# A hybrid block on one core: a re-planned instruction order, a fifth convolution on TensorE, and a routing in two branches

## The chip, the cores and the metric

The kernel runs on one core of a Trainium2 chip. The metric is the device time of one execution in microseconds. A core has five engines with their own in-order instruction streams: TensorE (PE) multiplies matrices, VectorE (DVE) and ScalarE (ACT) work element by element, GpSimd (POOL) does the same and helps out, and SyncE (SP) issues nearly all DMA transfers. Engines wait for one another through semaphores, so an instruction whose input is late holds everything behind it on its own engine.

## The reference

The input x is 8 sequences of 512 tokens with 128 features. Four residual layers follow one another, each on a layer-normalised input:

- attention A: a gated delta rule over 16 heads of size 8. Queries, keys and values are projections of the input, each followed by a causal convolution of four taps in time and a SiLU. A state of 8 x 8 per head is carried from token to token: `v_new = (v - k S) * beta; S = S + outer(k, v_new); o = q S`.
- a mixture of experts (MoE): logits over 8 experts, the two largest chosen, their softmax weights normalised; each expert is relu(x W1) W2 with W1 128 x 256 and W2 256 x 128. The reference computes all 8 experts for all tokens and weighs them.
- attention B: linear attention with elu + 1 as its feature map, causal, with a state of 8 x 9 per head from chunk to chunk.
- the same MoE again, with the same weights.

## The kernel before, in words

**Units.** The 512 tokens are cut into 8 units (`c`, 0 to 7) of 64 time steps (`CH`) of all 8 sequences: 512 tokens each, four tiles of 128. For each unit, in this order: `prepare` (layer norm, projections with convolution, normalised keys), `recurring` (the delta rule), `ending` (its output, written by the VectorE instruction `on` and passed over DRAM by two DMAs, `sco` and `oT`), then `f` (the first MoE), `b` (attention B) and `g` (the second MoE). The last unit is split into two halves from `f` on.

**The delta rule.** `recurring` walks through 16 steps of four tokens per unit. Each step is a chain of four VectorE instructions: `pj` (product), `factors` (sum), `terms` (product), `st` (sum), and the next step needs the `st` of this one. `substituted` prepares the four tokens of a step so that they can be taken together (its tiles are `W`, `spare` and `near`). GpSimd multiplies the outputs (`po`); they are summed by TensorE in the first three units, by VectorE in the others.

**Entering the MoE.** When `on` has come back through DRAM, TensorE multiplies it by the output weights (`s_po_a`, in `add_projected`) and VectorE adds it to x. That is the first TensorE instruction of `f`.

**The MoE.** For each expert, TensorE computes `s_ph` (two matmuls of 512 columns), ScalarE the relu (`hT`), TensorE `y_py` (two matmuls). The scaled input of an expert (`wt_xsT`) is made by GpSimd from weights that a DMA spreads over all partitions (`scw`). Expert weights lie in eight buffers `resident_0` to `resident_7`.

**The convolution.** With `TAPS_ON_PE = 4`, units 0 to 3 are convolved on TensorE: `weights_of_taps` multiplies the projection by each tap, and `convolved` issues four matmuls (`s_pp_a<-xnT_a,resident`) per projection. Units 4 to 7 are convolved by one matmul, two ScalarE instructions and three VectorE `scalar_tensor_tensor` per projection (`s_pp_a<-cv_a`). The tap weights `wc` lie in `resident_5` to `resident_7`, so that `loading_later_weights` must wait for the last tap matmul of unit 3 before it loads experts 5 to 7.

**Routing.** In `moe`, `first_of_largest` finds the largest logit and a one-hot mark of it, twice; then `relative` makes the two weights from the difference of the two largest logits (subtract, scale, tanh on ScalarE, two more on VectorE).

**Attention B.** In `attend`, GpSimd makes outer products of keys and values in the buffer `kv` (two instructions `kv_b`), TensorE sums them causally (`s_pc_b`), and VectorE multiplies by the queries (`qs_b`, `nd_b`).

**The order.** Nothing is scheduled on the chip, and the instruction order is not written out by hand either. The class `Weaver` runs the whole kernel as generators that name the engine of their next step, and takes at each point the generator that can start first, with ties and small differences decided by `chains` (length of work behind a step) and by offsets in `FAVOURED` and `OFFSETS`. Start times come from the prices in `duration()`, plus extra time booked by `weaver.took(...)`. `PLANS = 4` plans are made without instructions, and the last one fixes the order. The prices thus decide which instruction stands where on its engine; on the chip each engine then follows that order.

**Fill.** Where the planner sees TensorE idle for 0.6 us or more, `keep_busy` (line 1950) issues matmuls of ones by ones that compute nothing, for 0.7 of the gap, so many at a price of 0.22 us each. The profile shows them as `busy`.

Of the kernel before, what the change touches and what calls it, by code (L numbers as in the profile page):

```python
# [19 lines left out]
P = 128  # L20
# [17 lines left out]
TURNED = 1  # L38
# [3 lines left out]
TAPS_ON_PE = 4  # L42
# [4 lines left out]
ADDED_ON_DVE = (4,5,6,7)  # L47
NEAR_NORMS = (5,6,7)
# [5 lines left out]
TURNED_IN = (0,7)  # L54
# [13 lines left out]
PASSES = ()  # L68

FAVOURED = {  # L70
    ("b", 0.0): 1475, ("b", 1.0): -605, ("b", 2.0): 408, ("b", 3.0): -1141, ("b", 4.0): 1159, ("b", 5.0):
    -397, ("b", 6.0): -3095, ("b", 7.0): -2237, ("b", 7.5): -2071, ("beside",): 1509, ("ending",): 696,
    ("f", 0): 1839, ("f", 1): 922, ("f", 2): 673, ("f", 3): -941, ("f", 4): 1648, ("f", 5): 1050, ("f", 6):
    -1587, ("f", 7): 767, ("f", 7.5): -2892, ("g", 0.0): 1576, ("g", 1.0): 901, ("g", 2.0): 357, ("g", 3.0):
    7212, ("g", 4.0): -253, ("g", 5.0): -2424, ("g", 6.0): -246, ("g", 7.0): 1986, ("g", 7.5): -2626,
    ("outputs",): 7, ("prepare", 0): -904, ("prepare", 1): -3306, ("prepare", 2): 224, ("prepare", 3):
    -1571, ("prepare", 4): -839, ("prepare", 5): -16, ("prepare", 6): 680, ("prepare", 7): -2427, ("recur",
    0): 3219, ("recur", 1): -6342, ("recur", 2): -2844, ("recur", 3): 482, ("recur", 4): -2744, ("recur",
    5): -1405, ("recur", 6): 1064, ("recur", 7): -724, ("values",): 149, None: -1498,
# [4 lines left out]
    -5735, -5206, -179, -62, -5753, 0, -6219, -6323, 29, -6838, 1464, 2372, 2338, -2, 1277, -3446, -3136,  # L84
    2417, -3137, -2112, -3119, -3650, -311, 76, 1, 3, -3, 77, -342, -7970, 977, -20, -4091, 3665, -19, 806,
    -4343, -4621, -4648, -4379, 711, 806, -5289, 1734, 1900, 1275, 623, -5269, -420, -380, -832, -1479, 50,
    -758, -790, 125, -3620, 585, -553, 237, 2322, 2064, -5521, 501, -5381, -5928, -3498, -40, 2563, 4086,
    10628, -5495, 782, 11097, 2142, 524, -2998, -175, 1440, -9862, 334, 747, 94, -5047, -6796, 307, 308,
    -1787, -402, -3506, -63, -187, 265, -2927, -6059, -6411, -6618, 0, -4528, -6371, -6553, -6091, -5056,
    263, -538, -1107, -6503, -6983, -6, -6510, -36, -961, -967, 294, 389, -6742, -8230, -142, -7747, -8737,  # L90
    -7250, -7254, -7665, -422, 1935, 282, -996, -6683, -9031, 177, 1221, 466, 360, -7342, 552, -8817, -42,
    -7371, 101, 1699, 247, 245, 186, -7410, 57, 713, -5151, 127, -91, -80, -5933, 56, -6006, -6402, 412,
    -6116, -445, 35, 2434, -4925, -4928, -4874, -938, 1079, 406, -7960, 775, 519, -186, -183, -6551, -7752,
    -7695, -8113, 429, 2079, 1870, 73, 72, 717, 130, -428, -37, 347, 2267, 385, -69, 3340, -640, -367, 165,
    -831, -1483, 0, 486, -5539, -200, -199, -399, -34, 2547, -7582, -106, -2671, 11037, 1388, 1383, 1120,
    -962, 17, -1270, -6162, -175, -5673, 211, 50, -7246, -2444, -7484, -2599, -386, 24, -1456, -1295, -1542,
    449, 95, 3319, -2490, -5181, -17, 250, 1245, 968, 926, -3459, -1, -51, -7241, -6288, -40, -5786, 456, 0,
    2, -7292, 471, -361, -79, -6239, 1121, 209, 228, 171, -490, -335, -1339, -4313, -4533, -173, -162,
    -1885, -4676, -5235, -6460, -342, -6601, -6575, 266, 235, 4646, 4647, 78, -899, -7489, 388, -348, 4,
    2051, 1488, -3366, -170, -1594, -5834, -4738, -590, -6081, 2703, 771, 806, 2101, -1052, -4471, -334,  # L100
    10046, 384, -6869, -6546, 10224, -8058, 323, -1252, 463, 8950, 0, -8361, 1480, -113, -361, -8416, -9767,
    -47, -200, -9523, 27, -8517, -60, 66, -8349, -229, -9575, -9613, 177, 0, -516, 2087, 1808, 1102, -3472,
    -3462, -3444, -261, -48, -604, -199, 8924, -1499, -2626, 0, -5333, -68, 0, -3882, -1964, 1388, 1387,
    -3692, -5022, -5065, -555, 136, 6558, 1420, 1897, 1801, 9994, 299, 277, 324, -41, 8082, 391, 7156, 7157,
    -5841, -322, -1273, -5351, 627, 9366, -2233, -2747, 1391, 674, -7825, -11438, -30, 775, 2023, 1821,
    -1660, -376, -7698, 679, -3112, 1424, -5849, 0, -55, 151, -899, 680, -7529, -8147, 148, 896, 1077, 914,
    339, 108, 425, -1456, -5019, -1472, -477, 2580, -4207, -3854, -4163, -8696, -1145, -4645, -48, -435,
    -49, -441, -2007, 528, -6603, 2721, 2590, 71, 790, 1764, 678, -1104, -11, -8403, -631, -307, -17, 8979,
    -26, 111, 125, -3643, 387, 709, -7661, -6188, -1529, 52, -267, -2256, -1638, -163, -7464, -7718, -7716,
    -1060, 1984, -7251, 341, -416, 74, 246, 826, 0, -1331, 114, -9262, 817, -794, -1132, -4670, 22, 677,  # L110
    -1102, -247, -991, 5324, 1460, 7056, -68, 22, -4777, -5911, -267, -245, 0, -5384, 611, 1441, -3227,
    -3228, 7000, -4910, -4927, 8594, 7076, 656, 8970, 534, 0, -414, -452, 8696, 199, -1793, 526, 7399,
    -2385, -2142, -2082, 703, 601, -344, 673, 889, 675, -225, 700, 0, 1159, -2605, -52, 1613, 16, -121, 10,
    3158, 128, 131, -45, -73, 1613, -6492, -6728, -6847, 1627, -162, 2762, 283, 57, -585, 605, 1, -6681,
    -6644, -7468, 1614, -1785, -6492, 3296, -2793, 740, 1374, 1438, -5170, -5140, 909, 2571, -5016, 298,
    -5165, -4644, -50, -42, -4475, 2, 294, -85, -2740, -6839, 226, 1693, -57, 3901, -15, 128, 27, -353,
    1777, -988, 548, -1117, 51, -5550, -5713, 147, 12, -34, -4251, 1589, 1915, 47, -3918, 1053, 111, -9287,
    183, -73, -1509, -1272, -1576, 1611, -436, 1, 5846, -1241, -112, 1631, -1205, 1597, 150, -2745, -3535,
    2377, 2411, 1644, 1676, -1215, 1575, -4452, 8420, 702, -792, 816, 406, 430, 763, 8525, 846, -158, 8634,
    8574, 7499, -111, 1400, 1450, 1002, 8654, -2038, 769, 762, 607, 2855, 6551, -97, -90, -87, 5399, 647,  # L120
    -2965, 11537, -1025, 26, 1690, -128, 1901, -2876, -579, -1637, -1629, 2367, 1239, 1591, 19, 1583, 1724,
    11913, 9792, -979, -5647, 234, 2469, -6345, 305, -458, 202, 495, 2179, 331, -2292, 9691, 1045, 6, 9790,
    35, -5846, 323, 577, 1291, 9691, -58, -97, 118, -5, -4, 615, -5886, 76, -98, -106, -3895, 613, 2012,
    -4473, 833, 614, 2011, -59, -171, -3273, -3336, -3353, -3, -4885, 1032, 10012, 4, 9990, -8535, 13, -26,
    -426, 9852, -8409, 100, -8705, 1140, -1782, -3, -354, -197, -1938, -335, 9717, -197, 9802, 2602, -4020,
    6594, -4069, 2798, 3058, 2, -79, -78, 391, 1966, 1709, 200, 8716, 1885, 10615, 11418, 3662, 9797, 2272,
    1035, 2099, 0, 1824, 10195, 9823, 10532, 9755, 10009, 1333, 1142, -251, 8119, 297, 296, 41, 749, 4723,
    747, 1875, 2107, 724, -124, 453, 7278, 3607, 3799, 273, 3441, 3113, -3692, -398, -3768, -334, -3765,
    -3766, -582, -412, 9876, -382, 1211, 10712, -1001, 93, -1201, 9799, -302, 9584, 9796, 780, 9701, -580,
    1068, 9799, -828, -878, 2215, 2732, -4744, 3104, 2677, 2684, 2623, 238, -387, -153, 2284, -614, 2072,  # L130
    231, 2027, -4996, -71, 30, 457, -4797, 384, -249, 4030, 2190, -5523, 4173, 1217, 3083, 1929, -714, 605,
    676, -732, -321, -57, 3956, 733, 11526, -7059, -800, 1502, 239, -723, -808, -318, -541, 8037, -8544, 15,
    -4952, -5089, -5252, -4993, 2029, -304, -831, -5698, -69, -6182, -350, -409, 2461, 257, -282, -7155,
    -5747, 0, -11360, 2325, 2107, 2122, 386, -5700, -3106, -1352, 0, 0, -1541, 372, -1538, -3081, -1573,
    -1435, -66, 3013, -2727, -4066, -895, -131, -4357, 2917, -4077, -498, 0, -3157, -80, -404, -3201, -3374,
    0, 1576, 1292, 11286, -3695, -3696, 11437, 2265, 10445, 11425, 0, 3814, -3061, -6147, -44, -59, 400,
# [331 lines left out]
def duration(key, op, args, kw):  # L468
# [12 lines left out]
    if key == "ACT":  # L481
        table = TABLE_OF.get(args[2]) if op == "activation" else None
        scale = args[2] if op == "mul" else kw.get("scale", 1.0)
        more = (0.19 if "bias" in kw else 0.0) + (0.0 if isinstance(scale, float) else 0.08)
        return key, 0.2 + more + n * 0.76e-3, 0.1, table
# [1523 lines left out]
```

## Time and profile before

| | |
|---|---|
| median of 3 runs | 791.46 us (791.4 to 791.99) |
| profiled execution, its own time | 792.24 us |
| its span, first to last instruction | 790.5 us |
| mean granted TensorE clock | 0.989 |
| PE / DVE / ACT / POOL busy | 761.7 / 565.3 / 504.4 / 446.1 us |
| PE fill (`busy`), 195 matmuls | 54.4 us |
| DMA | 59.67 MB, 75 GB/s in the mean |

The page gives busy time by engine, the span in 40 slices, a chain of the work that ended last, and groups of like instructions. A row of a group reads: line, engine, operation, output and inputs by tile name, shapes, count, then busy time and the mean duration of one in ns, then the idle time just before them and what ended it. Almost all instructions carry line 454, a helper that records every operation; so groups are told apart by tile names. A tile that begins with `s_` or `y_` lies in a matmul bank. Windows give busy time within stretches that the reader chooses; waits list who waited for whom. An fp32 matmul shows as two records.

### The profile page before, as it was taken

How to read it: one execution, taken by the hardware profiler on the slowest of the kernel's cores; microseconds unless marked ns; L12 is line 12 of the kernel's file. 1: busy time of each engine (PE TensorE's matmuls, PEld its weight loads, DVE VectorE, ACT ScalarE, POOL GpSimd, SP SyncE). 2: the span in 40 equal slices, each digit the busy share in tenths (PEclk: the TensorE clock that was granted, in tenths of full speed). 3: DMA queues.
4: the chain of work that ended last, by engine and by line, in shares of the span. 5: the costliest groups of instructions: out<-in, count | busy, mean ns of one | idle time of the engine just before them, and what ended most of it. 6: DMA issues, size and time to landing. Idle time of an engine off the chain costs nothing.

```text
span 790.5 us, 11578 instructions
## 1 busy us (share of the span) xinstructions
PE 761.7 (96%) x3383; PEld 385.6 (49%) x3383; DVE 565.3 (72%) x1429; ACT 504.4 (64%) x1388; POOL 446.1 (56%) x609
## 2 busy tenths in 40 slices
PE   8889899997999999999999999999999999999997
PEld 4345455553435434544444435454444457644475
DVE  1689898978997799899999799798557155342310
ACT  5765767687876865678676875773664445643352
POOL 1245447659586495775586664877735606735331
PEclk9999899998999999999999999999999999999999
DMA  2451426105233311214133142232112111311121
GB/s 46 118 130 38 129 57 182 51 22 147 70 91 86 98 56 55 80 55 126 54 110 100 31 105 74 82 105 68 41 41 81 60 28 48 108 69 41 40 60 34
DMA packets 82392, 59.67 MB, mean 75 GB/s; under 512 B 48152, under 2 KB 64152, under 8 KB 82328
## 3 DMA queue, kind: packets, MB, share of 16 engines
q1 hardware_dynamic: 81608, 58.64, 26.5%
q8 instruction: 27, 0.44, 0.2%
q10 hardware_dynamic: 720, 0.28, 0.2%
q14 instruction: 37, 0.30, 0.1%
HBM read 46.52 MB, written 12.39 MB: 75 GB/s over the span
## 4 chain that ended last, share of the span: by engine, by line
PE 76%; DVE 13%; ACT 6%; issue 3%; DMA 1%; POOL 1%; DVEq 0%; SPq 0%; ACTq 0%; POOLq 0%
PE s_ph_f L454 14%; PE y_py_f L454 14%; PE s_ph_g L454 12%; PE y_py_g L454 12%; PE s_pc_b L454 4%; PE s_pp_a L454 4%; PE s_pp_b L454 2%; DVE st L454 2%; PE s_pu_b L454 2%; PE busy L1950 2%; PE s_pS_b L454 1%; DVE pj L454 1%; ACT squares L454 1%; DVE terms L454 1%; DVE W L454 1%
## 5 line engine op out<-in xcount | busy, mean ns | idle before, releaser
L454 ACT ACTIVATE hT_g<-s_ph_g 128x512 f32<-128x512 f32 (+1 forms) x144 | 79.0, 551 | 95.4 <-PE s_ph_g L454 94.5
L454 PE MATMUL y_py_f<-hT_f,resident 128*128 128x512 f32 (+1 forms) x288 | 134.3, 555 | 0.3 <-ACT hT_f L454 0.2
L454 PE MATMUL y_py_g<-hT_g,resident 128*128 128x512 f32 (+1 forms) x288 | 133.3, 553 | 0.3
L454 PE MATMUL s_ph_f<-wt_xsT_f,resident 128*128 128x512 f32 (+1 forms) x288 | 132.6, 555 | 0.8 <-ACT wt_xsT_f L454 0.2
L454 PE MATMUL s_ph_g<-wt_xsT_g,resident 128*128 128x512 f32 (+1 forms) x288 | 131.0, 553 | 0.3 <-POOL wt_xsT_g L454 0.2
L454 ACT ACTIVATE hT_f<-s_ph_f 128x512 f32<-128x512 f32 (+1 forms) x144 | 78.7, 549 | 50.1 <-PE s_ph_f L454 48.7
L454 POOL TENSOR_TENSOR wt_xsT_g<-wt_xsT_g,xn_xnT_g 128x512 f32<-128x512 f32 (+1 forms) x69 | 79.1, 1167 | 37.0 <-DMA wt_xsT_g<-scw_g 26.5
L454 POOL TENSOR_TENSOR po<-st,kq 128x256 f32<-128x256 f32 x128 | 93.9, 763 | 3.3 <-DVE st L454 2.7
L454 POOL TENSOR_TENSOR kv_b<-ph_b,v 128x1152 f32<-128x1152 f32 x32 | 69.2, 2177 | 40.3 <-ACT v L454 27.1
L454 POOL TENSOR_TENSOR wt_xsT_f<-wt_xsT_f,xn_xnT_f 128x512 f32<-128x512 f32 (+1 forms) x69 | 79.6, 1172 | 16.4 <-DMA wt_xsT_f<-scw_f 11.5
L454 DVE TENSOR_TENSOR qs_b<-s_pc_b,ph_b 128x360 f32<-128x360 f32 (+1 forms) x96 | 50.4, 551 | 46.4 <-PE s_pc_b L454 45.8
L454 PEld LDWEIGHTS y_py_f<-hT_f,resident 128*128 128x128 f32 x288 | 50.6, 190 | 47.5 <-issue 40.1
L454 PEld LDWEIGHTS s_ph_f<-wt_xsT_f,resident 128*128 128x128 f32 x288 | 50.5, 191 | 46.7 <-issue 31.1
L454 PEld LDWEIGHTS y_py_g<-hT_g,resident 128*128 128x128 f32 x288 | 50.9, 190 | 44.1 <-issue 35.6
L454 PEld LDWEIGHTS s_ph_g<-wt_xsT_g,resident 128*128 128x128 f32 x288 | 50.9, 190 | 43.7 <-issue 32.0
L454 DVE TENSOR_REDUCE st<-terms 128x64 f32<-128x320 f32 x128 | 61.5, 480 | 12.2 <-ACT terms L454 5.8
L1950 PE MATMUL busy<-ones 128*128 128x512 bf16 x195 | 54.4, 420 | 8.8 <-ACT o L454 2.6
L454 DVE TENSOR_REDUCE factors<-pj 128x32 f32<-128x288 f32 x128 | 58.5, 457 | 6.2 <-ACT factors L454 2.5
L454 DVE TENSOR_TENSOR terms<-factors,kt 128x256 f32<-128x256 f32 x128 | 53.7, 419 | 4.0 <-ACT vn L454 1.0
L454 DVE TENSOR_TENSOR pj<-st,factors 128x256 f32<-128x256 f32 x128 | 53.4, 417 | 4.2 <-ACT factors L454 1.5
L454 ACT COPY terms<-st 128x64 f32<-128x64 f32 x128 | 39.6, 309 | 26.2 <-DVE st L454 24.8
L454 POOL TENSOR_TENSOR pq<-y_a,y_a 128x128 f32<-128x128 f32 x32 | 20.9, 679 | 46.8 <-ACT squares L454 23.7
(270 smaller groups left out, 1342.7 us busy)
## 6 DMA issues: line engine op xcount, KB each, us to landing
wt_xsT_f<-scw_f SPq DMA_DIRECT2D x55, 256.0 KB
wt_xsT_g<-scw_g SPq DMA_DIRECT2D x55, 256.0 KB
scr<-y_a SPq DMA_DIRECT2D x24, 256.0 KB
qk<-scr SPq DMA_DIRECT2D x16, 256.0 KB
x_a<-in_x_dram SPq DMA_DIRECT2D x16, 128.0 KB
vv<-scr SPq DMA_DIRECT2D x8, 256.0 KB
sco<-on SPq DMA_DIRECT2D x8, 256.0 KB
oT<-sco SPq DMA_DIRECT2D x8, 256.0 KB
```

The source lines that it names most:

```text
L454: r = call(*args, **kw)
L1950: nc.tensor.matmul(pt, ones, ones.unsqueeze(1).to_broadcast([P, 4, P]), start=True, stop=True)
```

## The change

Five things are changed:

1. `TAPS_ON_PE` is 5: unit 4 is convolved on TensorE as well.
2. The tap weights lie in `kv`, the buffer of attention B's outer products, in place of the weights of experts 5 to 7. The loading of these experts no longer waits; instead the first `attend` waits for the last tap matmul of unit 4.
3. In the routing, `relative` is started as soon as the second largest logit is known, beside the rest of `first_of_largest`.
4. Prices of the planner are corrected: GpSimd's power function 0.4 + 0.16 per element with nothing booked on top (it was 1.05 and 0.8 more), other GpSimd operations, ScalarE's bias and scale, output products in the first units (0.08 in place of 0.3), two VectorE operations that are slower than their formula, and a burst of weight loads.
5. The order is planned anew: two kinds of passes (`PASSES`) follow the four plans, in which steps are placed backwards from the end, and `FAVOURED` and `OFFSETS` are replaced.

`STATES_ON_PE`, `KEYS_ON_POOL` and the code under them are switched off (empty tuples). `TURNED` names the same parts as before.

```diff
-TURNED = 1
+TURNED = {"f0": 1, "g0": 1, "f7": 1, "g7": 1}
-TAPS_ON_PE = 4
+TAPS_ON_PE = 5
+STATES_ON_PE = ()
+KEYS_ON_POOL = ()
+BURST = NE - 3
-TURNED_IN = (0,7)
-PASSES = ()
+PASSES = ((1, 0.0, {}), (2, 0.1, {}))
 FAVOURED = {
...
 OFFSETS = (
...
-        more = (0.19 if "bias" in kw else 0.0) + (0.0 if isinstance(scale, float) else 0.08)
+        more = (0.1 if "bias" in kw else 0.0) + (0.0 if isinstance(scale, float) else 0.06)
         return key, 0.2 + more + n * 0.76e-3, 0.1, table
     if key == "POOL" and ALU.pow in args:
-        return key, 1.05, 0.1
+        return key, 0.4 + n * 0.16, 0.1
     if key == "POOL":
-        return key, 0.2 + n * (1.72e-3 if n > 512 else 2.0e-3), 0.1
+        if op == "tensor_copy":
+            return key, 0.16 + n * 1.3e-3, 0.1
+        return key, 0.18 + n * (1.73e-3 if n > 512 else 2.15e-3), 0.1
...
-    wc = [resident[NE - 3 + s].rearrange("p (k d) -> p k d", k=4) for s in range(3)]
+    kv_ = const.tile([P, 2, NH, V1, HD], F32, name="kv")
+    taps = kv_.rearrange("p w h e d -> p (w h e d)")[:, 0 : 12 * D].rearrange("p (s k d) -> p s k d", s=3, k=4)
+    wc = [taps[:, s] for s in range(3)]
...
-    kvs = held_in(1, [P, 2, NH, V1, HD], "kv")
+    kvs = Slots(weaver, None, None, "kv", 1, [kv_])
...
         for e in range(NE):
-            if TAPS_ON_PE and e >= NE - 3:
-                yield fired("projected", TAPS_ON_PE - 1, e - (NE - 3))
...
                 sp.dma_start(resident[e][:, to], by)
+                if e >= BURST and to.stop < 2 * NF:
+                    weaver.moves(-LANDS)
...
         pool.tensor_tensor(rs[:, 0], rs[:, 0], mhalf, ALU.pow)
-        weaver.took("POOL", 0.8)
...
             dve.tensor_scalar(nrm[:, s], nrm[:, s], ATT_A_EPS * ATT_A_EPS, None, ALU.max)
+            weaver.took("DVE", 0.3)
...
+                weaver.took("DVE", 0.4 * ns / NS)
...
-                                weaver.took("POOL", 0.3)
+                                weaver.took("POOL", 0.08)
...
         def first_of_largest(p, k):
             m = near(nb) if k else row(f"m{k}")
             yield "DVE"
             dve.tensor_reduce(m, p, AX.X, ALU.max)
+            if k:
+                scales["weights"] = spawn(relative(m1, m))
             yield "DVE"
             dve.tensor_tensor(marked, p, over_experts(m), ALU.is_ge)
...
-        m2 = yield from first_of_largest(lg2, 1)
-        yield from relative()
+        yield from first_of_largest(lg2, 1)
+        yield scales["weights"]
...
         projecting = spawn(project())
         adding = spawn(elus())
+        if c == 0:
+            yield from all_of([fired("projected", TAPS_ON_PE - 1, s) for s in range(3)])
         kv = yield from kvs.take(n)
```

## The prediction

> **What bounds the kernel now.** I read the page first: busy shares by engine, then the span in 40 slices.
>
> ```profile
> span 790.5 us, 11578 instructions
> ...
> PE 761.7 (96%) x3383; PEld 385.6 (49%) x3383; DVE 565.3 (72%) x1429; ACT 504.4 (64%) x1388; POOL 446.1 (56%) x609
> ...
> PE   8889899997999999999999999999999999999997
> ...
> DVE  1689898978997799899999799798557155342310
> ```
>
> TensorE (PE) is busy all the time, but 195 of its matmuls are fill that computes nothing ("busy", line 1950). So I cut the span where PE starts the first product of a new unit (`s_po_a`, at 103.08, 153.87, 204.64 and 263.93 us for units 0 to 3) and asked for PE's busy time in each stretch:
>
> ```profile
> 0.00:103.08 103.08, 90.62 (x424) 0.95 0.36 91
> 103.08:153.87 50.79, 49.95 (x218) 1.00 0.39 107
> 153.87:204.64 50.77, 43.66 (x230) 0.93 0.31 81
> 204.64:263.93 59.29, 57.31 (x252) 1.00 0.32 88
> ...
> 740.00:790.50 50.50, 45.76 (x192) 0.99 0.19 48
> ```
>
> (length, PE busy with its count, granted clock, DMA share, GB/s), and for the fill alone (length, PE busy, weight-load busy, then the same):
>
> ```profile
> 0.00:103.08 103.08, 36.95 (x138) 14.39 (x138) 0.95 0.36 91
> 103.08:153.87 50.79, 3.83 (x14) 1.36 (x14) 1.00 0.39 107
> 153.87:204.64 50.77, 9.21 (x28) 3.22 (x28) 0.93 0.31 81
> ...
> sum 790.50, PE 54.36 PEld 20.45; mean PE 5.44 PEld 2.04
> ```
>
> Idle plus fill I call waste. It is 12.5 + 36.9 = 49.4 us in the first stretch, 4.7 in the second, 7.1 + 9.2 = 16.3 in the third, 2.4 in the fourth, 2.8 from 263.93 to 740 us and 4.7 + 2.8 = 7.5 at the end: 83.1 us. The other 707.4 us are real PE work. After 204.64 us PE hardly stops; a microsecond can be won only in real work, or in the 72.8 us wasted ahead of unit 3.
>
> What PE waits for there is VectorE (DVE). A unit enters PE's work when its recurrence has ended with the instruction `on`, which starts at 95.2, 145.05, 193.31 and 251.20 us for units 0 to 3; `s_po_a` follows 7.9, 8.8, 11.3 and 12.7 us later, over two DMAs. DVE is busy for 64.7, 45.8, 41.5 and 48.5 us of the four stretches that end with `on`. The largest DVE wait of the third:
>
> ```profile
> DVE s_pp_a L454 <- ACT s_pp_a L454: 4.3, 1, 4.3
> ```
>
> **The change part by part.** Durations are of the profiled execution, whose own time is 792.24 us (span 790.5 and 1.7 around it), 0.78 above the median 791.46. I add the change of the span to the median.
>
> *Convolution of unit 4 on TensorE.* The built programs have 12 more four-tap matmuls `s_pp_a` and 3 fewer single ones. The row:
>
> ```profile
> L454 PE MATMUL s_pp_a<-xnT_a,resident 128*128 128x512 f32 x96 | 42.9, 595 | 0.0
> L454 DVE SCALAR_TENSOR_TENSOR s_pp_a<-cv_a,cw,s_pp_a 128x512 f32<-128x512 f32 x36 | 26.8, 749 | 4.9 <-ACT s_pp_a L454 4.5
> ```
>
> Two records make one fp32 matmul, so one is 42.9 / 48 = 0.89 us; the chain of waits has 11 in a row in 9.54, 0.87 each. Nine more at 0.87 are +7.8 us of real work on the bounding engine (7.7 with the 0.86 of `s_ph` in a run, 8.1 with 12 x 0.89 less 3 x 0.86). DVE loses 9 x 0.749 = 6.7 us and a wait of up to 4.3; ScalarE loses three copies of about 0.58 and three scalings of 0.65, 3.7 us, none on PE's path; GpSimd six copies of 0.21. The part pays only through an earlier `on`, below.
>
> *Weights in the buffer `kv`.* Experts 5 to 7 no longer wait for the taps; the first outer product of unit 0's attention waits for the last tap matmul of unit 4. In the built order that matmul stands at 85 us of PE work and the first `s_pp_b` of the attention at 122, so 37 us of PE work cover the wait: nothing. Without that cover, GpSimd would hold its `po` products (0.79 us each) behind the waiting `kv`, and `st` buffers behind those. SP issues the same 379 instructions. The nine loads of these weights move ahead: in the order, three stand between `sco` and `oT` of unit 0, each 0.45 us of SP. `oT` waits there for `sco` to land anyway; if it did not, 1.4 us, once.
>
> *Routing.* Both orders have the same DVE instructions; subtract, scaling and tanh now overlap four operations of 0.19. At most 0.8 us for one of 18 routings, and only where PE waits for it (unit 0's, the last half's). Taken as nothing; bounds 0 and -1.6.
>
> *One more table load* on ScalarE (34 to 35 in the order): 1.28 us on an engine with 36% idle; nothing, +1.3 at most. The Trainium skill (ScalarE: Activation LUTs, What ACT_TABLE_LOAD costs) adds about 1.38 us of drain to each, 2.66 in all. Here the load at 14.40 us follows an activation that ends at 14.39, and the next starts at 15.74, so the drain does not show, and the row's value stands; by the page the bound would be +2.7.
>
> *The order.* Fill falls from 195 to 158: 127 ahead of unit 0's `s_po_a` (138 before), 22 in the second stretch (14), none in the third (28), 2 in the fourth (1), 7 later (14). What the waste becomes I take from DVE, with the durations of its rows summed over the built order up to each `on`. Before, these sums are 70.9, 120.9, 167.1 and 220.3; the busy time to the same points is 0.91 of that, since neighbours overlap. After: 64.7, 122.5, 158.9 and 248.1.
>
> Start: unit 0's keys are convolved in turn with its values; two matmuls stand ahead of the last one that the keys need, 1.7 us later for all that follows (bounds 0, if the table load at 14.40 covers it, and 1.7). `on` of unit 0: 95.2 - 0.91 x 6.2 + 1.7 = 91.3 us. Unit 1: 57.8 x 0.91 + 4.1 idle as before = 56.7 on, 148.0. Unit 2: 36.4 x 0.91 + 6.8 = 39.9 on, 187.9 (183.5 without the 4.3 wait). Unit 3: 89.2 x 0.91 + 9.4 = 90.6 on, 278.5; the order now has the preparation of two further units ahead of it (30 more instructions, 17.7 us) and 14 more of attention (8.7).
>
> PE work ahead of each `s_po_a`, by row sums of the order scaled to the trace (1.06): 53.7, 105.4, 143.3 and 224.2 us. Waste up to unit 0: 91.3 + 7.9 - 53.7 = 45.5. Unit 1: 148.0 + 8.8 - 105.4 = 51.4. Unit 2: 187.9 + 11.3 - 143.3 = 55.9, or nothing more if the wait goes; between them 53.6. Unit 3: 278.5 + 8.4 (the first two lags; the others had other PE work ahead) - 224.2 = 62.7, where it was 72.8. Bounds: 274.1 + 7.9 gives 57.8; DVE idle grown with its work (9.4 x 89.2 / 53.2 = 15.8) and a lag of 12.7 give 73.4. For units 4 to 6 the same sums stay below unit 3's. I take 62.7: the idle of the same stretch, the nearest row.
>
> End: 4 fills instead of 10, at 0.28 each 1.7 us; half is taken as gone, -0.8. Clock: the third stretch ran at 0.93; of its 34.5 us real work some 2.4 us is slow clock, and half of that goes with its gaps, -1.2 (0 to -2.4).
>
> Sum: +7.8 - 10.1 - 0.8 - 1.2 = -4.3 us: span 786.2, median **787.2 us**.
>
> The granted clock dips where PE has gaps: 0.95 and 0.93 in the rows above, 1.00 where it is full. The Trainium skill (TensorE: Matmul & The Clock Gate, Part 1) has the array fall to half rate after an idle window of about 3.4 us and need as much work to return. That speaks against dropping 37 fills: one such fall would cost about 1.7 us, an estimate from that page, and the sum by it would be -2.6; the longest PE wait ahead of a fill here is 2.3 us.
>
> **The rivals.** *DVE becomes the bound at unit 3.* The order moves 28 us of DVE work ahead of that `on`, and PE has no fill there. If `on` comes at 282.8 us, 4.3 later than summed, the gain is gone; at the upper bound (+10.7) the time is 797.9. For it: DVE is 8 or 9 tenths busy up to half the span, and its idle was wait for PE and ScalarE that the packed order may add to. Against: two prepared units make units 4 and 5 cheap.
>
> *Fill turns into idle.* The gaps stay but for 7.8 us, and the convolution eats that: 791.5. For it: the 12.5 idle us of the first stretch lie beside fill that was meant to cover them. Against: third stretch, where 16.3 us have a named cause on DVE.
>
> *The waste follows the fill.* 83.1 us for 195 fills is 0.43 each; 37 fewer are -15.8, with +7.8 it is -8.0: 783.5. For it: the new durations are near the rows (GpSimd's power function was priced 1.05 + 0.8, the row says 0.97; the new price is 1.04). Against: the 128 recurrence steps keep prices of 1.65 us for the four rows' 1.77.
>
> **How the numbers follow.** Forecast (785 to 790) 0.36; waste follows fill (779 to 785) 0.25; fill turns into idle (790 to 793) 0.17; DVE at unit 3 (793 to 798) 0.22. Range 779 to 797. About 0.2%, 1.6 us, is what can be told from no change: faster 0.60 (all but a rest of the first two), same 0.18, slower 0.22.
>
> **What would show it.** Right: waste of about 63 us up to unit 3's `s_po_a`, the third stretch under 5 us, real work near 715; `on` near 91, 148, 188 and 278 us. Wrong: `on` of unit 3 after 283; PE waits named on `s_po_a` or its addition; waste over 3 us between unit 3 and 740 us; a granted clock under 0.95 after 104 us.

## The result and the profile after

The changed kernel takes 802.38 us (median of 4 runs, 801.37 to 804.1); the kernel before took 791.73 us beside it. The ratio is 1.0125, with a 95% interval of 1.01 to 1.015: slower by 10.6 us, where 787.2 had been forecast. The profiled execution took 801.37 us with a span of 799.6 us, and the granted clock was 0.994 in the mean. The page's first part, busy time by engine:

```profile
span 799.6 us, 11526 instructions
...
PE 759.5 (95%) x3364; PEld 385.2 (48%) x3364; DVE 572.0 (72%) x1420; ACT 504.5 (63%) x1385; POOL 445.4 (56%) x603
```

The shares are those of before; what differs is within the stretches.

TensorE's busy time in the changed kernel, cut where the first product `s_po_a` of units 0, 1, 2 and so on starts (length, busy with its count, granted clock, DMA share, GB/s):

```profile
0.00:96.32 96.32, 84.92 (x411) 1.00 0.40 102
96.32:159.55 63.23, 59.27 (x262) 0.97 0.39 101
159.55:204.08 44.53, 37.63 (x183) 0.92 0.38 99
204.08:290.23 86.15, 83.87 (x399) 1.00 0.22 63
290.23:367.25 77.02, 76.90 (x327) 1.00 0.20 56
...
740.00:799.60 59.60, 53.68 (x220) 1.00 0.18 41
```

The fill alone, in the same windows (length, busy, weight-load busy, and so on):

```profile
0.00:96.32 96.32, 32.05 (x127) 12.42 (x127) 1.00 0.40 102
96.32:159.55 63.23, 5.08 (x22) 2.06 (x22) 0.97 0.39 101
159.55:204.08 44.53, 0.00 (x0) 0.00 (x0) 0.92 0.38 99
...
sum 799.60, PE 39.74 PEld 15.34; mean PE 3.97 PEld 1.53
```

Length less busy time, plus fill, is the waste: 43.4, 9.0, 6.9 and 2.9 us in the first four stretches, 62.3 in all where 72.8 were wasted before and 62.7 had been summed. So far the account holds. But both kernels start unit 2's `s_po_a` at the same time (204.08 and 204.64 us), and from there the new order takes 595.5 us, the old one 585.9. TensorE's real work from there is 575.1 us against 573.2; its waits and fill are 20.4 us against 12.7. So 7.7 of the 9.1 us by which the span grew are waits behind that point. Who waited for whom on TensorE between unit 3's `s_po_a` and 740 us, first in the changed kernel, then in the kernel before (total us, times, longest):

```profile
PE y_py_f L454 <- ACT hT_f L454: 2.8, 4, 0.9
PE s_pw_f L454 <- DVE cb_f L454: 1.8, 1, 1.8
PE s_pt_f L454 <- DVE x_a L454: 1.3, 1, 1.3
PE s_pty_g L454 <- ACT hT_f L454: 1.1, 2, 0.7
PE s_ph_f L454 <- ACT hT_f L454: 0.7, 1, 0.7
```

```profile
PE s_pw_f L454 <- DVE cb_f L454: 0.4, 1, 0.4
PE s_pt_b L454 <- DVE x_a L454: 0.3, 1, 0.3
```

Two kinds have grown: waits for a routing's result or for x on VectorE (`cb_f`, `x_a`; 3.7 us with the smaller entries, 0.7 before) and waits for the relu `hT` on ScalarE (4.9 us, 0.2 before). Of the first kind the trace shows the making. VectorE and then GpSimd around 656 us in the changed kernel (start, duration, engine, operation, and in brackets the idle time before it):

```profile
655.74 0.17 DVE L454 TENSOR_TENSOR y_pl_f<-y_pl_f,rs_f 128x2 f32<-128x2 f32 x1 [1.62 <-POOL rs_f L454]
656.22 2.12 DVE L454 SCALAR_TENSOR_TENSOR y_pl_f<-p_f,by_f 128x2 f32<-128x2 f32 x2 [0.31 <-ACT p_f L454]
658.37 0.20 DVE L454 TENSOR_TENSOR y_pl_f<-hots_f,y_pl_f 128x32 f32<-128x32 f32 x1
```

```profile
655.94 2.17 POOL L454 TENSOR_TENSOR kv<-ph_b,v 128x1152 f32<-128x1152 f32 x1
```

The two weighting operations of the routing work on two numbers per partition, and together they take 2.12 us. The first alone takes 1.92 us and ends at 658.14 us, when GpSimd's outer product `kv`, which ends at 658.11, has ended. There are 36 such operations. In the changed kernel 14 of them take over 0.2 us, and each of the 14 ends 0.02 to 0.03 us after a GpSimd operation has ended; in the kernel before there are nine, with the same ends. All 36 take 9.8 us in the kernel before and 14.8 in the changed one (`y_pl<-p,by`):

```profile
L454 DVE SCALAR_TENSOR_TENSOR y_pl_f<-p_f,by_f 128x4 f32<-128x4 f32 (+1 forms) x18 | 5.7, 314 | 0.7 <-ACT p_f L454 0.6
L454 DVE SCALAR_TENSOR_TENSOR y_pl_g<-p_g,by_g 128x4 f32<-128x4 f32 (+1 forms) x18 | 4.1, 230 | 2.6 <-ACT p_g L454 2.0 <-POOL oc L454 0.3
```

```profile
L454 DVE SCALAR_TENSOR_TENSOR y_pl_g<-p_g,by_g 128x4 f32<-128x4 f32 (+1 forms) x18 | 7.6, 422 | 0.5
L454 DVE SCALAR_TENSOR_TENSOR y_pl_f<-p_f,by_f 128x4 f32<-128x4 f32 (+1 forms) x18 | 7.2, 401 | 0.9 <-ACT p_f L454 0.5
```

VectorE up to `on` of units 1 to 3 in the changed kernel (length, busy, then as above). Before, the idle parts were 4.1, 6.8 and 9.4 us; now they are 8.5, 8.2 and 5.9:

```profile
87.88:150.19 62.31, 53.85 (x134) 0.97 0.39 101
150.19:191.14 40.95, 32.75 (x82) 0.97 0.35 94
191.14:280.59 89.45, 83.52 (x186) 0.98 0.22 60
```

### The profile page after: what moved, and what is told of

Read it like the earlier page. It is cut to its first block, busy times and chain, and to the rows that moved or that the text cites. A ratio compares the mean times of both kernels' runs of the same rounds, so it can differ in the third digit from the quotient of the medians.

```text
span 799.6 us, 11526 instructions
## 1 busy us (share of the span) xinstructions
PE 759.5 (95%) x3364; PEld 385.2 (48%) x3364; DVE 572.0 (72%) x1420; ACT 504.5 (63%) x1385; POOL 445.4 (56%) x603
## 4 chain that ended last, share of the span: by engine, by line
PE 72%; DVE 9%; ACT 8%; POOL 6%; issue 2%; DMA 2%; SPq 0%; DVEq 0%; POOLq 0%; ACTq 0%
PE s_ph_g L454 12%; PE y_py_g L454 12%; PE s_ph_f L454 11%; PE y_py_f L454 10%; PE s_pp_a L454 7%; PE s_pc_b L454 5%; ACT squares L454 3%; POOL wt_xsT_f L454 2%; PE s_pp_b L454 2%; PE s_pu_b L454 2%; PE busy L2007 1%; PE s_po L454 1%; PE s_pS_b L454 1%; DMA wt_xsT_f<-scw_f 1%; POOL rs_a L454 1%
## 5 line engine op out<-in xcount | busy, mean ns | idle before, releaser
L454 PE MATMUL s_ph_f<-wt_xsT_f,resident 128*128 128x512 f32 (+1 forms) x288 | 135.3, 566 | 8.5 <-POOL wt_xsT_f L454 6.9
L454 PE MATMUL y_py_g<-hT_g,resident 128*128 128x512 f32 (+1 forms) x288 | 133.8, 552 | 0.0
L454 POOL TENSOR_TENSOR kv<-ph_b,v 128x1152 f32<-128x1152 f32 x32 | 69.4, 2184 | 49.0 <-DVE ph_b L454 27.4
L454 PE MATMUL s_pp_a<-xnT_a,kv 128*128 128x512 f32 x120 | 54.6, 597 | 0.1
L454 POOL COPY st<-st 128x64 f32<-128x64 f32 x31 | 7.7, 248 | 70.7 <-DVE st L454 70.7
```

What stands on the lines that cost most here:

```text
L454: r = call(*args, **kw)
```

## The experiments

A planner that is run again after an edit gives quite another order, and then two things have changed. So each kernel below keeps the order of the changed kernel ("new order") or of the kernel before ("old order") step by step, and only the edit's own steps are laid in by hand. Times are medians; the new order itself spreads from 801.4 to 804.1 us, so 1.5 us are not told apart in it. Ratios are to the kernel before, which was run beside each and had medians of 791.8 to 794.5 us there.

**Two misses.** The convolution was first given back to VectorE in the new order, and moved to TensorE in the old one.

```diff
-TAPS_ON_PE = 5        # new order
+TAPS_ON_PE = 4
```

> The changed kernel's order kept step by step, but unit 4 convolved on VectorE again (tap weights stay in kv). Theory W (the nine added matmuls are paid in full on TensorE, the relief of VectorE buys nothing): 802.4 - 7.8 = about 794.5 us. Theory O (the new order costs the time, the convolution pays for itself as the forecast had it): VectorE gets 6.7 us and a wait of up to 4.3 back ahead of unit 2 and 3, 802 us or more. Between 796 and 800 both hold in part.

> The order of before kept step by step, but unit 4 convolved on TensorE, tap weights in kv. Theory W: 791.7 + 7.8 = 799.5 us. Theory O: the third stretch loses a part of its 16.3 us of waste, 788 to 792 us; no lower than its 28 fills allow.

Measured: 998.1 and 899.8 us. Both say nothing on the question: the edit adds or takes one step of the stream that prepares all units, and my alignment of the old and new steps slipped by one behind it, so that the later units' loads and norms came late (in the second kernel TensorE waited 60.1 us in seven waits for `xn_a`). They were made again, below.

**Do the nine matmuls cost what they take?** In the new order, three of the four taps of unit 4 are left out on TensorE.

```diff
-                for k in range(4):
+                for k in range(4 if c != 4 else 1):
```

> The changed kernel in its own order, with only the first of the four taps of unit 4 computed (9 of 12 matmuls left out, so unit 4's convolution is incomplete); nothing goes back to VectorE. It prices the nine matmuls alone. Theory W: 802.4 - 7.8 = 794.6 us. Rival (TensorE waits for VectorE at unit 3 in any case, so the matmuls lie in a gap): 800 to 802.5 us, with the idle time ahead of unit 3 longer by about 7 us.

Measured: 803.33 us, as with them. TensorE's busy time between the changed kernel's first two `s_po_a` fell from 59.3 to 53.8 us:

```profile
96.32:159.55 63.23, 53.80 (x244) 0.92 0.39 102
```

Unit 1's `on` stayed at 150.2, and idle took the place. Ahead of unit 2 a microsecond of TensorE's work is no microsecond of time.

**Does the wait at 188 us cost?** There TensorE waits 4.08 us for the last product of GpSimd that unit 1's experts need, made in the order 2, 1, 3, 0; here they are made in the order of need.

```diff
-# new order, unit 1's f: wt_xsT of experts 2, 1, 3, 0
+# 0, 1, 2, 3, in the same four places; the other routings alike
```

> The changed kernel's order, but the weight loads and GpSimd products of the first four experts of each routing trade places so that they go in the order in which TensorE needs them. In the changed kernel, unit 1's expert 0 comes last of four: TensorE idles 4.1 us for it at 188 us and then runs 7 us at about half clock (three matmuls in 4.45 us, where 2.6 are usual). Theory S (this stall is lost time): product 3.7 us earlier and no clock drop of 1.9 us, 797 us. Rival (VectorE sets the time of unit 3 anyway, the saved time comes back as a wait ahead of 290 us): 801 to 802.5 us.

Measured: 803.48 us, no gain. The 4.1 us wait is gone from the list, others (2.0, 1.8, 1.4 us) stand in its place.

**The convolution back on VectorE, once more.**

```diff
-TAPS_ON_PE = 5        # new order, the nine operations laid at unit 4's projections
+TAPS_ON_PE = 4
```

> The order of the changed kernel is kept; only the fifth unit's convolution goes back to VectorE. Theory F: nine VectorE operations of 0.75 us come back ahead of unit 3's outputs, which move from 280.6 to about 287, and the time is 807 to 811 us. Rival P: nine matmuls less, 794 to 797 us.

Measured: 813.88 us, ratio 1.0275 (1.026 to 1.0291), 2.9 us above the range of theory F. `on` of unit 1 comes at 160.2 us instead of 150.2, with VectorE 5.8 us busier and 3.7 us more idle up to it, and the 10 us stay to the end. In the new order, and with the nine operations in these places, this part of the change is worth 11 us.

**The convolution on TensorE in the old order**, first as one block, then in the places where only fill ran.

```diff
-TAPS_ON_PE = 4        # old order
+TAPS_ON_PE = 5
-    wc = [resident[NE - 3 + s].rearrange("p (k d) -> p k d", k=4) for s in range(3)]
+    wc = [taps[:, s] for s in range(3)]      # in kv, as in the change
```

> The order of the kernel before is kept step by step; only the fifth unit's convolution moves to TensorE, with its weights in the outer products' buffer (twelve matmuls in the places of its three projections, its nine VectorE operations gone). Theory F (the front, up to unit 3's outputs, is set by VectorE and the recurrence behind it; TensorE has room there): the nine operations of 0.74 us at 172.8 to 184.7 us of the profile before, and the 4.3 us that VectorE waited ahead of the first, go from VectorE's path, unit 3's outputs come 6 to 10 us earlier than 251.2, and the time is 782 to 787 us. Rival P (what counts is TensorE's work): nine matmuls more of 0.86 us, the time is 795 to 800 us.

> The order of the kernel before with the fifth unit's convolution on TensorE, its twelve matmuls in three groups of four laid where TensorE only ran filling matmuls at 172.9, 179.5 and 183.6 us of the profile before (those fillings are left out), not as one block of 7.1 us ahead of the attention's projections as in the run that cost 14 us. Theory G (the price of the matmuls is only that of their place): 786 to 792 us. Rival (the twelve matmuls or the shared buffer cost the front wherever they stand): 797 to 806 us.

Measured: 805.9 and 805.85 us (ratio of the second 1.0162, 1.013 to 1.0193). The first lies above what either theory had said. In it the matmuls also stood behind a ScalarE copy that I had laid too late; the second has that mended, and comes out the same, in the rival's range. VectorE is 5.6 us less busy from `on` of unit 1 to that of unit 2 and 8.6 us more idle. VectorE there in the second kernel:

```profile
145.43:196.79 51.36, 35.93 (x95) 0.93 0.25 69
```

What was taken off VectorE came back as waits for ScalarE and TensorE (up to `on` of unit 3: 6.2 us for `s_po_b`, where it was 4.0, and 5.1 for `factors` and 4.5 for `mn_b`, where they were under 0.4). One of these chains can be followed in the trace:

```profile
186.97 0.60 ACT L784 ACTIVATE y_a<-s_pp_a 128x512 f32<-128x512 f32 x1 [2.53 <-PE s_pp_a L784]
190.06 0.69 DVE L784 TENSOR_TENSOR ph_b<-s_pp_b,mn_b 128x512 f32<-128x512 f32 x1 [4.45 <-ACT mn_b L784]
190.89 2.17 POOL L784 TENSOR_TENSOR kv<-ph_b,v 128x1152 f32<-128x1152 f32 x1 [5.30 <-DVE ph_b L784]
```

The last group of tap matmuls ends at 186.9 us. ScalarE waits for it with the SiLU `y_a`, the exponential `mn_b` stands behind that in its queue, VectorE waits for `mn_b` and GpSimd for VectorE. The buffer `kv`, which the taps share with the outer products, is not what holds here: the first `kv` starts 4 us after the last tap matmul, when `ph_b` has ended. The same part of the change is worth -11 us in one order and +14 in the other. That the nine VectorE operations lie on the path of the old order has been refuted.

**Is any one engine's work the bound?** Three kernels of the new order leave work out of one engine alone: nine VectorE operations ahead of unit 2's `on`, twelve ahead of unit 3's, and fourteen matmuls of TensorE behind it.

```diff
                 for k in range(3):
                     yield "DVE"
+                    if c == 5:
+                        continue
```

> The order of the changed kernel; the nine VectorE operations of unit 5's convolution are left out (its output lacks three of the four taps; nothing else is changed). They stand at 178.8 to 191.2 us, ahead of unit 2's outputs at 191.1 and of unit 3's at 280.6. Theory F: both move 6 to 7 us earlier and the time is 795 to 797 us. Rival P, or a front set by another engine: 801 to 803 us.

```diff
-            for i in range(2):      # and the loop over j behind it
+            for i in range(2 if c not in (4, 5) else 0):
```

> The order of the changed kernel; in the back substitution of units 4 and 5, which stands between unit 2's and unit 3's outputs (191.1 to 280.6 us), the products with the first two keys and the four last multiply and add operations are left out: twelve VectorE operations, 10.3 us by their rows in that stretch (four at 1.21 us, eight at 0.68), and no work of another engine. Those two units' outputs are then not the reference's. Theory V (in that stretch VectorE, 93% busy, sets unit 3's outputs, and these set the end): the stretch shrinks from 89.5 to 79 to 81 us and the time is 792 to 794 us. Rival C (a chain through several engines' queues sets it, as the unchanged time without unit 5's nine operations suggests for the stretch ahead): VectorE gets idle instead, and the time is 800 to 803 us.

```diff
                 yield "PE"
+                if name != "f3" or i in (0, 2 * NE - 1):
                 pe.matmul(py[:, 0 : nb * P], ...)
```

> The order of the changed kernel; in unit 3's f routing fourteen of the sixteen second products of the experts (y_py, 128x512, 0.86 us apart in a row of them) are left out, so that unit's result lacks them. They stand behind unit 3's attention output at 290 us, where TensorE is busy 99% of the time. Theory T (from unit 2's s_po_a at 204 us on, which both kernels reach at the same time, TensorE's work and its waits are the time): 12 us less, 789.5 to 791.5 us. Rival C (a chain through the other engines sets it there too, as it does ahead of 204 us): 4 us less or fewer, 798 us or more.

Measured: 802.28, 800.89 and 800.37 us; all three are where the rivals put them. The profiled executions of the last two took 803.4 and 804.6 us. VectorE in the second, between `on` of units 2 and 3:

```profile
192.11:282.24 90.13, 76.21 (x174) 0.96 0.22 59
```

VectorE does 76.2 us of work instead of 83.5, and the stretch is 90.1 us long instead of 89.5. In the third, the stretch from unit 3's `s_po_a` to unit 4's shrank by 2.4 us for 12 us of matmuls, and TensorE's idle in it grew from 0.1 to 5.7. So neither VectorE at 93% nor TensorE at 99% is alone the bound: the chain of waits goes through several queues, and what one engine saves it waits for another. The trace shows such a chain at 129 us: GpSimd has the four short operations of a layer norm ahead of a product that the experts need, TensorE waits for that product, ScalarE for TensorE, and a copy for the recurrence stands behind that relu:

```profile
129.73 3.13 PE L454 MATMUL s_ph_f<-wt_xsT_f,resident 128*128 128x512 f32 x4 [2.84 <-POOL wt_xsT_f L454]
132.90 0.60 ACT L454 ACTIVATE hT_f<-s_ph_f 128x512 f32<-128x512 f32 x1 [2.04 <-PE s_ph_f L454]
133.39 0.30 ACT L454 COPY terms<-st 128x64 f32<-128x64 f32 x1
133.72 0.49 DVE L454 TENSOR_REDUCE st<-terms 128x64 f32<-128x320 f32 x1 [1.39 <-ACT terms L454]
```

**What holds the weighting operations?**

```diff
-            apart, p2 = near(nb), row("p2")
+            apart, p2 = near(nb), near(nb)     # near() lies in PSUM, row() in SBUF
```

> The order of the changed kernel; in the routings the half tanh that ScalarE writes (p2) lies in the routing's PSUM bank instead of SBUF, so that VectorE's 36 weighting operations of 128x4 read one operand from SBUF and not two. In the profile after they take 0.15 us at least and 2.18 us at most, 14.8 us in all against 9.8 before, and the long ones end when a GpSimd operation beside them ends. Theory L (they are held by GpSimd's operation): all take about 0.17 us, 6 to 7 us in all, TensorE's waits for cb at 658.9 and 770.6 us shrink from 1.8 and 1.25 us to under 0.6 each, and the time is 798.5 to 800.5 us. Rival: they wait for something that the operand's place doesn't touch, durations and time stay (801 to 803 us).

Measured: 797.65 us (796.38 to 799.04), 4.7 us under the changed kernel, with a ratio of 1.0074 (1.0058 to 1.009) against 1.0125 (1.01 to 1.015). The operations in that kernel:

```profile
L778 DVE SCALAR_TENSOR_TENSOR y_pl_g<-y_pl_g,by_g 128x4 f32<-128x4 f32 (+1 forms) x18 | 3.0, 167 | 0.5
L778 DVE SCALAR_TENSOR_TENSOR y_pl_f<-y_pl_f,by_f 128x4 f32<-128x4 f32 (+1 forms) x18 | 3.0, 165 | 0.8 <-ACT y_pl_f L778 0.5
```

None takes over 0.171 us any more. The wait for `cb_f` is gone from TensorE's list, that for `x_a` at 512 us too, and waits and fill between unit 3's `s_po_a` and 740 us fall from 10.4 to 6.7 us. That is the largest piece of the loss that a run gave back.

The same edit in the old order:

> The order of the kernel before; only the half tanh of the routings lies in PSUM. Theory L (GpSimd's operation holds VectorE's when both of VectorE's operands are in SBUF): the 36 weighting operations go from 9.8 to about 6 us, but TensorE's wait for cb at 612.9 us is only 0.43 us and the others are covered, so the time falls by 0.3 to 1.5 us, to 790.3 to 791.5 us; the side by side routing of the changed kernel is then what laid these operations beside GpSimd's. Rival: as much as in the changed order, 4 to 5 us, 787 us.

Measured: 791.5 us against 792.5, ratio 0.9984 (0.9968 to 1.0), 12 runs: no more than the 0.2% that can just be told. The old order had 3.9 us of such holding, nearly all of it covered; the new one has 8.8, and pays for about half. That it is the side by side routing which laid these operations beside GpSimd's is not shown: the two orders differ in everything else as well, and no run has one without the other. With the matmuls of the convolution in the gaps as well:

> The last but one edit and the last together: order of the kernel before, matmuls of the fifth unit in the gaps, half tanh in PSUM. By theories G and L 785 to 791.5 us, under the kernel before; by the rivals 796 to 805 us.

Measured: 802.14 us, in the rivals' range. That is 3.7 us less than without the half tanh, but the intervals overlap (1.0091 to 1.0139 after 1.013 to 1.0193); the convolution still costs 10.6 us.

**The waits for `hT`.** The exponentials of attention B are left out, on top of the half tanh.

```diff
-            yield "exp"
-            act.activation(mn, mn, AF.Exp, scale=-1.0)
```

> The order of the changed kernel with the half tanh in PSUM; besides, the sixteen exponentials of the linear attention on ScalarE (0.63 us each) are left out, and with them four loads of its function table (1.28 us each), so the attention's features are not the reference's. Theory Q (TensorE's remaining waits for hT behind unit 3, 4.5 to 5 us, come of ScalarE's queue, which is 82% busy at 354 to 417 us): those waits fall under 2.5 us, and the time is 793.5 to 796 us against 797.65. Rival (they come of TensorE's own order, a second product straight behind its first): waits and time stay, 796.5 to 798.5 us.

Measured: 796.53 us, and TensorE's waits for `hT` in that kernel, 290 to 740 us:

```profile
PE y_py_f L779 <- ACT hT_f L779: 2.2, 3, 1.0
PE s_pty_g L779 <- ACT hT_f L779: 1.0, 2, 0.7
PE s_ph_f L779 <- ACT hT_f L779: 0.7, 1, 0.7
```

4.2 us remain of 4.9 (all entries for `hT`), with 15 us less on ScalarE, and the time is the same within its interval (ratio 1.0061, 1.0031 to 1.009, after 1.0074). So these 15 us of ScalarE's load are not their cause. One of the waits can be read in the changed kernel's timeline: TensorE's order has a second product `y_py` straight behind the `s_ph` that it needs (at 411.9 and 413.9 us, 0.93 us of wait), the relu lies between them, and nothing else is laid there. That the others are alike was not tested.

**VectorE's wait in the second branch.** In the new order VectorE meets, at 169.2 us, the multiply by `rs_f` that now stands beside the rank operations, and waits; the recurrence's `st` is queued behind it:

```profile
172.27 0.17 DVE L454 TENSOR_TENSOR y_pl_f<-y_pl_f,rs_f 128x4 f32<-128x4 f32 x1 [3.06 <-POOL rs_f L454]
172.35 0.48 DVE L454 TENSOR_REDUCE st<-terms 128x64 f32<-128x320 f32 x1
```

The squares from which `rs_f` comes stand on ScalarE behind two `kq` copies and two relus; they are taken ahead of these, alone and with the half tanh.

```diff
-# new order, ScalarE: square, kq copy x2, relu x2, square x3
+# square x4, kq copy x2, relu x2
```

> The order of the changed kernel; only the three squares of unit 1's f routing that ScalarE issues behind two kq copies and two relus (at 169.3 us) are taken ahead of those, next to the first square at 166.0 us. In the profile after, VectorE stands 3.06 us, from 169.2 to 172.3 us, at the multiply of the routing's second branch (it needs rs_f, which GpSimd makes of the squares), and the recurrence's st stands behind it. Theory S (this wait, which the side by side routing put into VectorE's queue, sets the front): the wait is under 0.5 us, unit 2's s_po_a comes 2 to 3 us earlier, and the time is 799 to 800.5 us. Rival (the copies and relus moved back cost as much, or another queue sets the front): 801.5 to 804 us.

> The same edit together with the half tanh in PSUM. Theory S: the two add up, 794 to 796 us. Rival: 797 to 799 us, as with the half tanh alone (797.65).

Measured: 803.54 and 799.58 us (ratios 1.0141 and 1.0083), no gain. VectorE in the first of them:

```profile
170.62 0.17 DVE L778 TENSOR_TENSOR y_pl_f<-y_pl_f,rs_f 128x4 f32<-128x4 f32 x1 [0.36 <-POOL rs_f L778]
173.39 0.48 DVE L778 TENSOR_REDUCE st<-terms 128x64 f32<-128x320 f32 x1 [2.60 <-ACT p_f L778]
```

The first wait is gone and another of nearly its size stands one instruction later, at the end of the same ScalarE queue: `terms` and `p_f` are now the ones behind the copies and relus. Taking this wait away was no gain by itself.

**Less on ScalarE there.** Six `kq` copies of units 3 to 5 go to GpSimd, in both orders, with the half tanh.

```diff
-                yield "ACT"
-                act.copy(kq[:, s]...)
+                yield "POOL" if c in (3, 4, 5) else "ACT"
+                (pool.tensor_copy if c in (3, 4, 5) else act.copy)(kq[:, s]...)
```

> The order of the changed kernel with the half tanh in PSUM; besides, the kq copies of units 3, 4 and 5 (six, 1.13 us each on ScalarE) are GpSimd's, in the same places of the order. Theory A (ahead of unit 2's s_po_a the recurrence waits for copies that stand in ScalarE's queue: its load sets the front): two of the copies stand at 166.4 to 168.5 us, right ahead of the squares and of the copy that the recurrence's st waits for; the front is 2 to 3 us earlier and the time 794 to 796 us against 797.65. Rival (the front has no one engine that sets it, or GpSimd's added 6 to 7 us cost as much): 797 to 800 us.

> The same two edits in the order of the kernel before. Theory A: 788 to 790.5 us, under both kernels. Rival: 791 to 794 us, as the half tanh alone (791.5).

Measured: 800.97 and 801.63 us, where the kernel before took 794.5 beside them: ratios 1.0088 (1.0057 to 1.0119) and 1.0099 (1.0068 to 1.013), after 1.0074 and 0.9984 with the half tanh alone. Nothing is gained in the new order, and some 9 us are lost in the old one. GpSimd in the first of them:

```profile
121.63 1.11 POOL L780 COPY kq<-qk 128x512 f32<-128x512 f32 x1 [8.66 <-DMA qk<-scr]
122.58 0.24 POOL L780 COPY st<-st 128x64 f32<-128x64 f32 x1
122.78 3.04 POOL L780 TENSOR_TENSOR po<-st,kq 128x256 f32<-128x256 f32 x4
```

GpSimd came to the copy early and stood 8.66 us for its DMA, with the recurrence's copy and products behind it. So these two runs price a new wait and leave open what a lighter ScalarE queue would bring.

## Why the prediction was wrong

The span was summed as 786.2 us and is 799.6. By the prediction's own terms (us):

| term | summed | measured | difference |
|---|---|---|---|
| `on` of units 0, 1, 2, 3 | 91.3, 148.0, 187.9, 278.5 | 87.9, 150.2, 191.1, 280.6 | -3.4, +2.2, +3.2, +2.1 |
| unit 3's `s_po_a` | 286.9 | 290.2 | +3.3 |
| waste up to there | 62.7 | 62.3 | -0.4 |
| waste from there to 740 | 2.8 | 10.4 | +7.6 |
| waste from 740 to the end | 6.7 | 7.1 | +0.4 |
| real work, clock included | 714.0 | 719.8 | +5.8 |

The 13.4 us that the sum missed are 7.6 us of waste behind unit 3 and 5.8 us of real work; the two other differences cancel. Of the 5.8, 0.7 are the matmuls (+8.5 and not +7.8), 1.2 the clock term, and 3.9 are matmuls that both kernels have and that were busy longer in the new order.

**The step that failed** is a term put at nothing without a reason: the waste from unit 3's `s_po_a` to 740 us stayed at 2.8 us in the sum. The prediction looked there at the arrival of new units alone ("For units 4 to 6 the same sums stay below unit 3's"), because TensorE had hardly a wait there before. But the whole order was laid anew, and an engine that is 99% busy in one order is so because that order was free of waits. The runs showed 10.4 us in its place, and the waits are inside the units: 3.7 us for routing results and x on VectorE, 4.9 for the relu. The first kind went when the weighting operations were freed (10.4 to 6.7 us); what makes the second is open but for the one wait read above.

**The routing** was "Taken as nothing; bounds 0 and -1.6". Only the saving was looked for. What was not asked is what stands beside the weighting operations on GpSimd in the new order. Freeing them gave back 4.7 us in the new order and at most 0.3% in the old one, so a cost stood where the bounds allowed none. How much of it comes of the routing in two branches and how much of the new order as a whole, no run tells apart. The rows for it were there: the kernel before shows the same operation at 0.15 and at 1.23 us. That VectorE would wait in its queue for `rs_f` was not said either; the experiments show that this wait hid another.

**The start and the front.** Unit 0's `on` came 3.4 us earlier than summed: the 1.7 us for the convolution's turn did not come, and VectorE's busy time to that point was 57.0 us. The gain was lost before unit 1's `on`: I took 4.1 us of VectorE's idle as before, and it was 8.5, by chains like the one at 129 us. The waste up to unit 3 is nevertheless what was summed, and that is luck: unit 3's `s_po_a` came 3.3 us later than summed, and TensorE had 3.7 us more work done by then.

**The nine matmuls**, +7.8: the rows nearly agree (`s_pp_a` 64.0 us after 55.5, +8.5), but the term does not belong into the sum, since taking them out again changed nothing. In this order the convolution on TensorE is a gain of 11 us, in the old one a loss of 14; the prediction's "the part pays only through an earlier `on`" was right, and no row sum could tell how much earlier.

**The clock**, -1.2: not gained, and there was next to nothing to gain. The prediction took 2.4 us of the third stretch's real work for slow clock. In the kernel before the granted clock was 0.50 from 185.7 to 192.5 us, and TensorE's work there was fill but for 0.15 us (first all of it, then the fill alone):

```profile
185.70:192.50 6.80, 5.43 (x13) 0.50 0.13 41
185.70:192.50 6.80, 5.28 (x12) 0.50 0.13 41
```

The third stretch ran at 0.92 (0.93 before), and without fill the slow clock now falls on real work. By such windows 6.7 us of real work ran at 0.50 ahead of unit 3 in the new order and 3.8 in the old one; half the difference, 1.4 us, is an estimate of the clock's part in the 3.9 us above, and the rest is open. The changed kernel's row: TensorE idle, then six records of `s_ph_f`, which took 2.92 us in the kernel before at 192.15 us; the granted clock stands behind TensorE's busy time in the windows:

```profile
192.01 4.45 PE L454 MATMUL s_ph_f<-wt_xsT_f,resident 128*128 128x512 f32 x6 [4.08 <-POOL wt_xsT_f L454]
```

```profile
190.00:192.00 2.00, 0.00 (x0) 0.50 0.09 20
192.00:194.00 2.00, 1.99 (x3) 0.50 0.35 131
...
196.00:198.00 2.00, 2.00 (x6) 1.00 0.97 208
```

The Trainium skill (TensorE: Matmul & The Clock Gate, Part 1) has the array at half rate after some 3.4 us of idle: this row agrees, with 0.50 after 4.08 us. The fall took 1.5 us of TensorE's time, near the 1.7 estimated from that page, but the run that removed the wait was no faster. The prediction's argument that no wait ahead of a fill was longer than 2.3 us did not protect either kernel: the fall at 185.7 us in the kernel before came with no longer wait than that ahead of it.

**The weights in `kv`**, nothing: right. GpSimd's first `kv` starts at 206.8 us and waits 3.1 us for `ph_b`; the last tap matmul had started at 148.8.

**The rivals.** "DVE becomes the bound at unit 3" named the right side and the wrong cause: `on` came before the 282.8 us from which it was to decide, and twelve VectorE operations less did not help. Two of the signs that were named for being wrong did show: waste over 3 us behind unit 3, and a clock under 0.95 after 104 us. Of the signs for being right, the third stretch kept 6.9 us of waste and not under 5, and real work was 719.8 and not near 715. The range ended at 797 because every case in it kept the second half of the kernel as it was.

What stays open is which queue would have to be freed for the front to come earlier. Work taken from VectorE, from TensorE and a wait taken from VectorE did not do it; ScalarE was not tried cleanly.

## What to carry to other kernels

When a whole order is planned anew, the stretch that had no waits is no safer than the rest: its waits must be looked for in the new order too, or left in the range. Row sums of one engine give neither the price nor the gain of moved work where the queues of four engines hold one another up; the same convolution on TensorE was worth -11 and +14 us in two orders. Before small VectorE operations are moved, look at what GpSimd does beside them, and keep one of their operands out of SBUF.

## What the runs showed of the hardware

A VectorE operation with two operands in SBUF was held up to 2.18 us, for 0.17 us of work, until a GpSimd operation on SBUF beside it had ended; with one of the operands in PSUM all 36 took 0.15 to 0.17 us. Not every GpSimd operation holds: at 676.24 us in the changed kernel the same operation took 0.16 us in the midst of GpSimd's power function `rk_b` (0.71 us). The Trainium skill (SBUF — State Buffer, Who interferes with whom) has the rule behind it: a VectorE instruction with two SBUF inputs contends with a GpSimd instruction that reads SBUF, and the ports that they share are locked exclusively. I had not looked for it at operations of two to four numbers per partition, where the holding is more than ten times the work.

TensorE's matmuls after an idle of 4.08 us ran at a granted clock of 0.50 for some 3 us, and it was at 1.00 again at 196 us. The clock also fell after less idle than the 3.4 us of the clock gate's page: it was 0.50 from 130.4 to 133.8 us in the changed kernel, after 2.84 us. The first `on` of the same order came between 87.9 and 91.6 us in the profiles of its variants, which shifts the whole rest: differences under 1.5 us between kernels of the new order are not read here.
